# Building a graph's adjacency blocks: a fixed window of 20 targets per tile, or 12 targets placed from the data

## The chip, the cores and the metric

The kernel runs on one core of a Trainium2 chip, in one launch. The metric is the device time of that core in microseconds (us). Five engines work side by side, each with its own instruction queue: TensorE (PE in the profile, its weight loads PEld), VectorE (DVE), ScalarE (ACT), GpSimd (POOL) and the DMA-issuing SyncE (SP).

## The reference, cut to what matters

A graph of 625 nodes with 512 features and 20,000 edges, sorted by target node `dst`, goes through four message-passing layers, each `x = x + layer(relu(norm(x)))`. The first two need, for each target, a sum over its edges:

```python
# layer 0: a mean of neighbours
neighbor_sum   = segment_sum(h[src], dst, n)
neighbor_count = segment_sum(ones, dst, n)
# layer 1, twice: 4 bases, 8 edge types
m   = sum_b comp[etype, b] * (h @ basis[b])[src]
agg = segment_sum(m * edge_weight, dst, n)
```

The edges are the same in both layers, so the sums are products with matrices that are built once: `cnt` (how many edges go from source to target) and eight weighted matrices `adj` (two sublayers, four bases), each 625 x 625.

## The kernel before, in words

The edges lie in 160 tiles of 125 (`NT`, `P`), in order of target. A tile's targets are near 625/160 = 3.9 times its number (`PACE`), give or take 8 (`SLACK`). The prologue in `tile_gnn` tests that for every edge; the number of offenders, `n_far`, selects the ordered body or a general one.

In the ordered body, `layers01_near` builds the matrices before any layer runs. First `coefficients` forms, in three calls of four, four and two slices, each edge's eight coefficients, and splits each into three bf16 parts whose sum is the f32 value; with a constant one for the count that is 25 columns per edge (`parts`). Then 20 steps (`s`) take eight tiles each, in two halves of four (`G`):

- VectorE makes `eq`, for each tile a comparison of its targets with the 20 (`W`) from a fixed start `low[t]`, and multiplies it with the 25 columns into `rh` (L441): 4 x 25 x 20 elements per half.
- VectorE makes `ohs` (L450), a one-hot of the tile's sources over five chunks of 128.
- TensorE multiplies them, for each tile five chunks by three parts (L455), into five PSUM tiles `q`, one per chunk, at the tile's offset. Eight PSUM tiles exist, so a step needs two that the step before has to give back.
- The windows of neighbouring steps overlap. VectorE adds the overlapping columns into `adj` and `cnt` (L466); ScalarE copies the new columns (L467).

After step 0 the loads of `x` and of later weights are queued (`load_rest`, `layer2_weights`); at steps 10 and 11 `x` is normalised (`norm_stats`, `norm_relu`). Then layer 0 starts with transposes of `h` (L213), the counts `pc` (L491) and the neighbour sums (L502). The order within an engine is that of a scheduler, except where `keep` pins an instruction behind the one before it on its engine.

Of the kernel before, what the change touches and what calls it, by code (L numbers as in the profile page):

```python
# [9 lines left out]
F32 = mybir.dt.float32  # L10
F16 = mybir.dt.float16
I32 = mybir.dt.int32
AF = mybir.ActivationFunctionType
# [17 lines left out]
SILU_2MOM = 1.679177  # L31
PACE = P * N / E
SLACK = 8


def locals_of(v):
    return [v[k] for k in "src_i dst_i src_f dst_f ew ea4 x iota_f ident ones eps two row iota_s rel_no mine et_r comp".split()]


@with_exitstack  # L40
def tile_gnn(ctx: ExitStack, tc: tile.TileContext, a: dict, out: bass.AP):
    nc = tc.nc
    const = ctx.enter_context(tc.tile_pool(name="const", bufs=1))

    with tc.tile_pool(name="temp", bufs=1) as temp:
        src_i = const.tile([P, NT], I32, name="src_i")
        dst_i = const.tile([P, NT], I32, name="dst_i")
        ew = const.tile([P, NT], F32, name="ew")
# [57 lines left out]
        nc.vector.reduce_sum(mine, blk, axis=mybir.AxisListType.X)  # L106


        dst_f = const.tile([P, NT], F32, name="dst_f")
        nc.vector.tensor_copy(dst_f, dst_i)  # L110
        off = temp.tile([P, NT], F32, name="off")
        nc.vector.scalar_tensor_tensor(off, tile_f, -PACE, dst_f, op0=ALU.mult, op1=ALU.add)
        out_lo = temp.tile([P, NT], F32, name="out_lo")
        nc.vector.tensor_scalar(out_lo, off, -float(SLACK), None, op0=ALU.is_lt)
        nc.vector.tensor_scalar(off, off, PACE + SLACK, None, op0=ALU.is_gt)
        nc.vector.tensor_add(off, off, out_lo)
        n_out = const.tile([P, 1], F32, name="n_out")
        nc.vector.reduce_sum(n_out, off, axis=mybir.AxisListType.X)
        far = const.tile([1, 1], I32, name="far")
        with tc.tile_pool(name="flag", bufs=1, space=bass.MemoryType.PSUM) as fp:  # L120
            pf = fp.tile([128, 512], F32, name="pf")
            nc.tensor.matmul(pf[:1, :1], n_out, ones, start=True, stop=True)
            nc.vector.tensor_copy(far, pf[:1, :1])
        src_f = const.tile([P, NT], F32, name="src_f")
        nc.vector.tensor_copy(src_f, src_i)
        nc.vector.tensor_copy(iota_s, src_no)
        n_far = nc.values_load(far, min_val=0, max_val=E)
    with tc.If(n_far < 1) as ordered:
        gnn_body(tc, a, out, locals_of(locals()), True)
    with ordered.Else():  # L130
# [13 lines left out]
def gnn_body(ctx: ExitStack, tc: tile.TileContext, a: dict, out: bass.AP, consts, near: bool):  # L144

    nc = tc.nc
    (src_i, dst_i, src_f, dst_f, ew, ea4, x, iota_f, ident, ones, eps, two, row, iota_s, rel_no,
     mine, et_r, comp) = consts
    sfx = "n" if near else "g"
    node = ctx.enter_context(tc.tile_pool(name=f"node{sfx}", bufs=1))  # L150
    work = ctx.enter_context(tc.tile_pool(name=f"work{sfx}", bufs=2))
# [227 lines left out]
    def layers01_near(wts2):  # L379
# [1 line left out]


        NQ = 2 * NB
        W = 20
        NS = NT // (2 * G)
        BF16 = mybir.dt.bfloat16
        low = [min(max(math.ceil(t * PACE - SLACK), 0), N - W) for t in range(NT)]
        with tc.tile_pool(name="adjacency", bufs=1) as bp:
            adj = bp.tile([P, NC, NQ, N], F32, name="adj")
            with tc.tile_pool(name="counts", bufs=1) as cp:  # L390
                cnt = cp.tile([P, NC, N], F32, name="cnt")
                with tc.tile_pool(name="build", bufs=2) as lp, \
                        tc.tile_pool(name="ps_build", bufs=8, space=bass.MemoryType.PSUM) as pp:

                    T = 128 // R
                    K = NT // T
                    cd = lp.tile([128, T, NQ], F32, name="cd", bufs=1)
                    nc.vector.tensor_mul(cd, mine[:, :, None].to_broadcast([128, T, NQ]),  # L400
                                         comp.rearrange("p l b -> p (l b)")[:, None, :].to_broadcast([128, T, NQ]))
                    oh_r = lp.tile([128, K, P], F32, name="oh_r", bufs=1)

                    parts = lp.tile([P, NT, 3 * NQ + 1], BF16, name="parts", bufs=1)
                    nc.gpsimd.memset(parts[:, :, NQ:NQ + 1], 1.0)
                    by_k = parts.rearrange("p (t k) q -> p k t q", k=K)
                    ew_k = ew.rearrange("p (t k) -> p k t", k=K)
                    keep = tc.keep_in_program_order

                    def coefficients(k0):  # L410
                        ks = slice(k0, min(k0 + 4, K))
                        n = ks.stop - k0
                        keep(nc.vector.tensor_scalar(oh_r[:, ks, :], et_r[:, ks, :], rel_no, None,
                                                     op0=ALU.is_equal))
                        p = pp.tile([128, 4, T, NQ], F32, tag="q", name="pco")
                        for k in range(n):
                            nc.tensor.matmul(p[:P, k], oh_r[:, k0 + k, :], cd, start=True, stop=True)
                        co = lp.tile([P, 4, T, NQ], F32, tag="co", name="co")[:, :n]
                        keep(nc.vector.tensor_mul(co, p[:P, :n],
                                                  ew_k[:, ks, :, None].to_broadcast([P, n, T, NQ])))  # L420
                        for i in range(3):
                            q0 = i * NQ + (i > 0)
                            v = by_k[:, ks, :, q0:q0 + NQ]
                            keep(nc.vector.tensor_copy(v, co))
                            if i < 2:
                                keep(nc.vector.tensor_sub(co, co, v))

                    coefficients(0)
                    end = 0
                    for s in range(NS):  # L430
                        b0 = low[s * 2 * G]
                        wd = low[(s + 1) * 2 * G - 1] + W - b0
                        q = [pp.tile([128, NQ + 1, 48], F32, tag="q", name="q") for _ in range(NC)]
                        for i in range(2):
                            eq = lp.tile([P, G, W], BF16, tag="eq", name="eq")
                            rh = lp.tile([P, G, 3 * NQ + 1, W], BF16, tag="rh", name="rh", bufs=3)
                            t0 = (2 * s + i) * G
                            for j in range(G):
                                nc.vector.tensor_scalar(eq[:, j, :], iota_f[:, low[t0 + j]:low[t0 + j] + W],
                                                        dst_f[:, t0 + j:t0 + j + 1], None, op0=ALU.is_equal)  # L440
                            keep(nc.vector.tensor_mul(  # L441
                                rh, eq[:, :, None, :].to_broadcast([P, G, 3 * NQ + 1, W]),
                                parts[:, t0:t0 + G, :, None]
                                .to_broadcast([P, G, 3 * NQ + 1, W])))
                            if s == 0:
                                coefficients(4 + 4 * i)
                            for j in range(G):
                                t = t0 + j
                                os_ = lp.tile([P, NC, 128], BF16, tag="ohs", name="ohs", bufs=6)
                                nc.vector.tensor_scalar(os_, iota_s, src_f[:, t:t + 1], None, op0=ALU.is_equal)  # L450
                                o = low[t] - b0
                                for c in range(NC):
                                    for k in range(3):
                                        q0, n = k * NQ + (k > 0), NQ + (k == 0)
                                        nc.tensor.matmul(q[c][:, :n, o:o + W], os_[:, c, :],  # L455
                                                         rh[:, j, q0:q0 + n, :],
                                                         start=i + j + k == 0,
                                                         stop=i == 1 and j == G - 1 and k == 2,
                                                         skip_group_check=True)

                        old = max(end - b0, 0)
                        for c in range(NC):
                            for dst, v in ((adj[:, c, :, b0:b0 + wd], q[c][:P, :NQ, :wd]),
                                           (cnt[:, c, None, b0:b0 + wd], q[c][:P, NQ:, :wd])):
                                if old:
                                    nc.vector.tensor_add(dst[:, :, :old], v[:, :, :old], dst[:, :, :old])  # L466
                                nc.scalar.copy(dst[:, :, old:], v[:, :, old:])  # L467
                        end = b0 + wd
                        if s == 0:
                            load_rest()  # L470
                            w2s = layer2_weights(wts2)
                        if s == NS // 2:
                            h = node.tile([P, NC, D], F32, tag="h", name="h")
                            stats = [norm_stats(c, keep) for c in range(NC)]
                        if s == NS // 2 + 1:
                            for c in range(NC):
                                norm_relu(h, c, stats[c], keep)
# [1028 lines left out]
```

## Time and profile before

| | us |
|---|---|
| median of three runs (1879.14 to 1885.42) | 1883.51 |
| the profiled execution, its own time | 1883.0 |
| its span in the profile | 1881.2 |
| PE busy over the span | 1772.1 (94%) |
| DVE busy over the span | 1074.1 (57%) |
| POOL busy over the span | 809.9 (43%) |
| first product of step 0 to first product of step 1 | 21.68 to 34.58 |
| first product of step 19 | 211.28 |
| first transpose of layer 0 | 221.42 |

The shares over the span mix stages with different limits. The adjacency build is the stretch up to about 220 us; what a change to it is worth has to be read from that stretch.

### The profile page before, as it was taken

Reading aid. Unit: us, or ns where it says so; the run is one execution under the profiler, and the core shown is the slowest. Engines: PE = TensorE matmul, PEld = TensorE weight load, DVE = VectorE, ACT = ScalarE, POOL = GpSimd, SP = SyncE. Lnnn points to the kernel's source line nnn. Section 1 sums busy time; section 2 is a strip of 40 time slices with the busy share of each in tenths; the row PEclk is TensorE's granted clock in tenths of the full one; section 3 lists DMA queues with packets and bytes.
Section 4 is the critical chain, followed back from the end, with each engine's and each line's share of the span. In section 5 each row is a group of like instructions: output and inputs, shape, how many; then the busy total and the mean of one; then the engine's idle time right before and its main releaser. Section 6 shows DMA issues by size and latency. Waiting matters only on the chain.

```text
span 1881.2 us, 25801 instructions
## 1 busy us (share of the span) xinstructions
PE 1772.1 (94%) x10688; PEld 960.7 (51%) x10688; DVE 1074.1 (57%) x1877; ACT 741.3 (39%) x856; POOL 809.9 (43%) x478
## 2 busy tenths in 40 slices
PE   5999999999999999999999989999999999999993
PEld 5999844444444444445455444444454444545441
DVE  8999611001100267768774657786676676666655
ACT  1122211000000312222221766767776777668670
POOL 0000000000000077556543688888887888788200
PEclk9999999999999989999999989999999999999996
DMA  2000103003000176565443589666675666666200
GB/s 70 2 2 2 52 0 140 0 0 93 2 0 0 30 187 162 139 146 161 125 119 98 116 150 172 127 122 119 109 132 114 115 132 116 109 119 125 36 0 13
DMA packets 157223, 162.68 MB, mean 86 GB/s; under 512 B 97546, under 2 KB 104059, under 8 KB 157096
## 3 DMA queue, kind: packets, MB, share of 16 engines
q0 software_dynamic: 131584, 119.48, 32.4%
q1 hardware_dynamic: 20100, 32.69, 5.7%
q10 hardware_dynamic: 5412, 8.77, 1.7%
q8 instruction: 86, 1.41, 0.3%
q14 instruction: 41, 0.34, 0.1%
HBM read 155.11 MB, written 5.12 MB: 85 GB/s over the span
## 4 chain that ended last, share of the span: by engine, by line
PE 83%; DVE 11%; ACT 2%; DMA 2%; issue 1%; POOL 0%; DVEq 0%; SPq 0%; ACTq 0%; POOLq 0%
PE z L1243 29%; PE agg L557 9%; PE hb L544 7%; PE sum L856 7%; PE tpw L834 5%; DVE rh L441 4%; PE z L1224 4%; PE z L1229 4%; DVE ohs L450 2%; PE agg L1267 2%; PE xsd L932 2%; PE mlp L786 2%; PE agg L533 2%; PE l L509 2%; PE nsum L502 1%
## 5 line engine op out<-in xcount | busy, mean ns | idle before, releaser
L1243 PE MATMUL z<-wm,z 128*125 128x512 f32 x1280 | 556.9, 593 | 2.7 <-DVE z L1362 2.7
L1243 PEld LDWEIGHTS z<-wm,z 128*125 128x125 f32 x1280 | 237.5, 188 | 293.5 <-issue 268.8
L230 POOL DMA_INDIRECT g_s<-xs,src_i x160 | 303.4, 1896 | 126.1 <-issue 75.5
L230 POOL DMA_INDIRECT g_s<-xd,dst_i x144 | 300.6, 2087 | 43.9 <-issue 42.0
L798 POOL MEMSET mT<- 128x5000 f32 x1 | 4.3, 4267 | 633.4 <-PE agg L557 633.4
L230 POOL DMA_INDIRECT gup<-up,src_i x160 | 198.1, 1238 | 132.0 <-DVE msg L841 60.6
L455 PE MATMUL q<-rh,ohs 125*128 125x160 bf16 (+1 forms) x2400 | 184.5, 238 | 13.5 <-ACT cnt L467 11.0
L455 PEld LDWEIGHTS <-ohs 125*128 125x128 bf16 x2400 | 180.0, 99 | 17.8 <-issue 15.0
L1245 DVE TENSOR_TENSOR mess<-z,b 125x512 f32<-125x512 f32 x160 | 106.4, 687 | 136.4 <-PE z L1243 136.4
L557 PE MATMUL agg<-hb,adj 125*125 125x512 f32 x400 | 173.6, 592 | 0.0
L547 DVE COPY hb<-hb 125x512 f32<-125x512 f32 x20 | 13.8, 692 | 261.0 <-PE hb L544 261.0
L856 PE MATMUL sum<-msg,ohy 125*32 125x128 f32 (+1 forms) x2560 | 146.0, 303 | 8.5 <-issue 6.9
L841 DVE TENSOR_TENSOR msg<-tpw,gup 125x768 f32<-125x768 f32 x160 | 152.0, 950 | 0.0
L856 PEld LDWEIGHTS sum<-msg,ohy 125*32 125x32 f32 x2560 | 101.2, 109 | 86.7 <-issue 85.7
L1231 DVE TENSOR_SCALAR z<-z,b 128x500 f32<-128x500 f32 (+1 forms) x164 | 108.4, 719 | 59.4 <-PE z L1229 57.5
L544 PE MATMUL hb<-basis,hT 128*125 128x512 f32 x320 | 138.6, 592 | 0.0
L1191 ACT ACTIVATE uz<-uz 128x2000 f32<-128x2000 f32 (+1 forms) x41 | 75.0, 1830 | 153.0 <-DVE uz L1183 153.0
L557 PEld LDWEIGHTS agg<-hb,adj 125*125 125x125 f32 x400 | 74.8, 188 | 94.7 <-issue 94.7
L549 ACT COPY hb<-hb 125x512 f32<-125x512 f32 x20 | 11.7, 586 | 258.3 <-PE hb L544 238.4
L839 DVE TENSOR_TENSOR msg<-tpw,gup 125x256 f32<-125x256 f32 x160 | 67.0, 419 | 62.9 <-PE tpw L834 31.1
L1191 ACT ACTIVATE um<-um 125x2048 f32<-125x2048 f32 x39 | 74.6, 1912 | 71.1 <-DVE um L1183 71.1
L544 PEld LDWEIGHTS hb<-basis,hT 128*125 128x125 f32 x320 | 60.1, 188 | 77.3 <-issue 76.8
(187 smaller groups left out, 2240.5 us busy)
## 6 DMA issues: line engine op xcount, KB each, us to landing
rt<-in_edge_attr SPq DMA_DIRECT2D x76, 125.0 KB
basis<-in_L_gnn_basis SPq DMA_DIRECT2D x8, 1024.0 KB
gup<-up,src_i POOLq DMA_INDIRECT x160
g_s<-xs,src_i POOLq DMA_INDIRECT x160
g_s<-xd,dst_i POOLq DMA_INDIRECT x144
w<-in_L_gnn_W SPq DMA_DIRECT2D x2, 1024.0 KB
loop<-in_L_gnn_loop SPq DMA_DIRECT2D x2, 1024.0 KB
w1ab<-in_L_gnn_W ACTq DMA_DIRECT2D x1, 2048.0 KB
```

Source lines behind the costliest of these rows:

```text
L230: return nc.gpsimd.indirect_dma_start(out=dst, out_offset=None, in_=table, in_offset=bass.IndirectOffsetOnAxis(ap=idx[:, t:t + 1], axis=0) ...
L441: keep(nc.vector.tensor_mul(rh, eq[:, :, None, :].to_broadcast([P, G, 3 * NQ + 1, W]), parts[:, t0:t0 + G, :, None] .to_broadcast([P, G, 3 ...
L455: nc.tensor.matmul(q[c][:, :n, o:o + W], os_[:, c, :], rh[:, j, q0:q0 + n, :], start=i + j + k == 0, stop=i == 1 and j == G - 1 and k == 2 ...
L544: nc.tensor.matmul(p[:P, :], hT[:, k, s * P:(s + 1) * P], basis[b][:, k, :], start=k == 0, stop=k == KD - 1)
L557: nc.tensor.matmul(acc[c], adj[:, s - 1, l * NB + b, c * P:(c + 1) * P], hb[:, b, :], start=False, stop=s == NC and b == NB - 1)
L834: nc.tensor.matmul(p[:P, :], hid[s // 2][s % 2][rws, i * P:(i + 1) * P], w4[rws].rearrange("p k u -> p (k u)"), start=True, stop=True)
L841: nc.vector.tensor_mul(m[:, :, 1:, :], pv[:, 2:4, None, :].to_broadcast([P, 2, 3, MUL]), g[:, None, 1:, :].to_broadcast([P, 2, 3, MUL]))
L856: nc.tensor.matmul(A[r * W:(r + 1) * W, c * MUL:c * MUL + v.shape[1]], oh[:, j, q, :], v, start=j % G == 0 and r not in done, stop=j % G = ...
L1191: keep(nc.scalar.activation(u, u, AF.Exp))
L1231: keep(nc.vector.tensor_scalar(zv[:, n, f, :], pf[f][:, :ne], b1[:, f:f + 1], None, op0=ALU.add))
L1243: nc.tensor.matmul(p[:P, :], z[:, j // w, f, j % w * P:(j % w + 1) * P], wm2[:, f, :], start=f == 0, stop=f == KD - 1)
L1245: keep(nc.vector.tensor_add(m[:, j, :], p[:P, :], bc["b2"]))
```

## The change

Twelve targets per tile in place of 20. Each group of eight tiles gets a base, worked out in the prologue from the target of the first edge of its fifth tile; a tile's 12 targets start at the base plus four (`STEP`) times its place in the group, so a group spans 40 targets (`WS`). Positions relative to that start (`rel`) are kept in a free part of `x`, and edges that fall outside the 12 are counted into `n_far` too. Two short products share one PSUM pool there.

Since the base is data, a step's 40 columns are written at an address from a register. `adj` and `cnt` are zeroed first (GpSimd: `cnt` and chunks 0 to 2; ScalarE: chunks 3 and 4), and every step is added in place. ScalarE copies `q` to `got` in SBUF and GpSimd adds it, for all five chunks in even steps; in odd steps VectorE adds chunks 3 and 4 from PSUM itself. The adding of a step is queued in the middle of the next. The comparisons `eq` are made for many tiles at once (`hots`). Of the one-hots of sources five are kept in place of six.

```diff
+NS = NT // (2 * G)
+STEP = 4
+WT = 12
+WS = (2 * G - 1) * STEP + WT
...
+        nc.tensor.matmul(pb[:, :NS], top, by_s[:, :, G], start=True, stop=True)
+        nc.vector.tensor_sub(rel, by_s, step_f)
...
+        nc.vector.tensor_scalar(base_f, pb[:, :NS], -float(STEP * G + (WT - STEP) // 2), 0.0,
+                                op0=ALU.add, op1=ALU.max)
+        nc.vector.tensor_scalar_min(base_f, base_f, float(N - WS))
+        nc.vector.tensor_copy(base_i, base_f[:1, :])
+        nc.vector.tensor_sub(rel, rel, base_f[:P, :, None].to_broadcast([P, NS, 2 * G]))
+        flat_rel = rel.rearrange("p s j -> p (s j)")
+        nc.vector.scalar_tensor_tensor(off, flat_rel, 0.0, off, op0=ALU.is_lt, op1=ALU.add)
+        nc.vector.scalar_tensor_tensor(off, flat_rel, WT - 1.0, off, op0=ALU.is_gt, op1=ALU.add)
...
-        low = [min(max(math.ceil(t * PACE - SLACK), 0), N - W) for t in range(NT)]
...
+                    def hots(t0, t1):
+                        keep(nc.vector.tensor_tensor(
+                            eq[:, t0:t1, :], iota_f[:, None, :WT].to_broadcast([P, t1 - t0, WT]),
+                            flat_rel[:, t0:t1, None].to_broadcast([P, t1 - t0, WT]), op=ALU.is_equal))
+
+                    hots(0, G)
+                    keep(nc.gpsimd.memset(cnt, 0.0))
+                    keep(nc.gpsimd.memset(adj[:, :3], 0.0))
+                    for c in range(3, NC):
+                        keep(nc.scalar.activation(adj[:, c], iota_f[:, None, :].to_broadcast([P, NQ, N]),
+                                                  AF.Copy, scale=0.0))
...
+                    def moved(s, eng):
+                        loads, (at,) = nc.values_load_multi_w_load_instructions(
+                            base_i[:1, s:s + 1], engines=(eng,), min_val=0, max_val=N - WS,
...
+                    def added(s):
+                        q = done.pop(s)
+                        lo, hi = STEP * (s == NS - 1), WS - STEP * (s == 0)
+                        n = NC - 2 * (s % 2)
+                        got = lp.tile([P, NC, NQ + 1, WS], F32, tag="got", name="got")[:, :n]
+                        for c in range(n):
+                            nc.scalar.copy(got[:, c, :, lo:hi], q[c][:P, :, lo:hi])
+                        at = moved(s, mybir.EngineType.Pool)
+                        for dst, v in ((adj[:, :n, :, at][:, :, :, lo:hi], got[:, :, :NQ, lo:hi]),
+                                       (cnt[:, :n, at][:, :, lo:hi], got[:, :, NQ, lo:hi])):
+                            keep(nc.gpsimd.tensor_add(dst, v, dst))
+                        if n < NC:
+                            at = moved(s, mybir.EngineType.DVE)
+                        for c in range(n, NC):
+                            for dst, v in ((adj[:, c, :, at][:, :, lo:hi], q[c][:P, :NQ, lo:hi]),
+                                           (cnt[:, c, at][:, lo:hi], q[c][:P, NQ, lo:hi])):
+                                keep(nc.vector.tensor_add(dst, v, dst))
...
-                            for j in range(G):
-                                nc.vector.tensor_scalar(eq[:, j, :], iota_f[:, low[t0 + j]:low[t0 + j] + W],
-                                                        dst_f[:, t0 + j:t0 + j + 1], None, op0=ALU.is_equal)
...
-                                os_ = lp.tile([P, NC, 128], BF16, tag="ohs", name="ohs", bufs=6)
...
-                        old = max(end - b0, 0)
-                        for c in range(NC):
-                            for dst, v in ((adj[:, c, :, b0:b0 + wd], q[c][:P, :NQ, :wd]),
-                                           (cnt[:, c, None, b0:b0 + wd], q[c][:P, NQ:, :wd])):
-                                if old:
-                                    nc.vector.tensor_add(dst[:, :, :old], v[:, :, :old], dst[:, :, :old])
-                                nc.scalar.copy(dst[:, :, old:], v[:, :, old:])
...
+                                hot.append(lp.tile([P, NC, 128], BF16, tag="ohs", name="ohs", bufs=5))
+                                nc.vector.tensor_scalar(hot[j], iota_s, src_f[:, 2 * s * G + j:2 * s * G + j + 1],
+                                                        None, op0=ALU.is_equal)
+
+                                if j == 1:
+                                    for cs in (range(3), range(3, NC)):
+                                        counted(0, cs)
+                                        counted(1, cs)
+                                elif j > 1:
+                                    counted(j, range(NC))
+                            if i == 0 and s > 0:
+                                added(s - 1)
+                        if s == NS - 1:
+                            added(s)
```

`rh` and the products are as before with 12 in place of 20: `rh` has 4 x 25 x 12 elements per half, the products 108 and 96 columns in place of 180 and 160.

## The prediction

> **What bounds the kernel now.** I read the page first. TensorE is busy nearly everywhere, so its share says nothing about a single stage; the rows of slices do (40 slices of 47 us). In slices 2 to 4 VectorE is at 8 or 9 tenths as well, and GpSimd is idle until slice 14.
>
> ```profile
> PE   5999999999999999999999989999999999999993
> DVE  8999611001100267768774657786676676666655
> POOL 0000000000000077556543688888887888788200
> ```
>
> That stretch is the adjacency build. The busy time of each engine in a window inside it, and the groups of instructions by shape up to 340 us:
>
> ```profile
> 85.00:125.00 40.00, 37.25 (x492) 36.38 (x490) 39.35 (x120) 8.19 (x41) 0.00 (x0) 1.00 0.01 2
> L455 PE MATMUL q<-rh,ohs 125*128 125x160 bf16 x1600 | 181.8, 236 | 0.0
> L455 PE MATMUL q<-rh,ohs 125*128 125x180 bf16 x800 | 179.3, 243 | 13.5 <-ACT cnt L467 11.0 <-DVE rh L441 2.4
> L441 DVE TENSOR_TENSOR rh<-eq,parts 125x2000 bf16<-125x2000 bf16 x40 | 89.4, 2237 | 0.1
> L450 DVE TENSOR_SCALAR ohs<-iota_s,src_f 125x640 bf16<-125x640 f16 x160 | 54.9, 382 | 0.3
> L439 DVE TENSOR_SCALAR eq<-iota_f,dst_f 125x20 bf16<-125x20 f32 x160 | 27.5, 232 | 0.0
> L466 DVE TENSOR_TENSOR adj<-q,adj 125x128 f32<-125x128 f32 x75 | 18.8, 286 | 3.9 <-PE q L455 3.9
> ```
>
> VectorE has no gap (39.35 of 40 us, clock 1.00 throughout), TensorE is close behind. In the chain of waits ordinary steps alternate rh, ohs, eq and the adds of L466: VectorE carries them. One step in the timeline:
>
> ```profile
> 55.16 8.82 PE L455 MATMUL q<-rh,ohs 125*128 125x180 bf16 x119 [0.65 <-ACT cnt L467]
> 57.63 2.24 DVE L441 TENSOR_TENSOR rh<-eq,parts 125x2000 bf16<-125x2000 bf16 x1
> 59.78 0.97 DVE L450 TENSOR_SCALAR ohs<-iota_s,src_f 125x640 bf16<-125x640 f16 x3
> 64.76 8.89 PE L455 MATMUL q<-rh,ohs 125*128 125x180 bf16 x119 [0.78 <-ACT cnt L467]
> ```
>
> Steps start 9.6 us apart here, 9.86 at most among plain ones; I take 9.7. TensorE streams 120 products at 8.82/119 = 74 ns and then waits 0.65 to 0.8 us for PSUM that VectorE and ScalarE still hold. By start-to-start distance VectorE's step is two rh of 2.15, eight ohs of 0.297, eight eq of 0.141, and ten adds with their gaps, 1.8: 4.3 + 2.4 + 1.1 + 1.8 = 9.6. It is full by itself.
>
> **The change, part by part.**
>
> *It takes the ordered body still.* The reference's own edges, put through the new arithmetic, give relative positions from exactly 0 to exactly 11: no edge is outside, n_far stays 0.
>
> *VectorE's step.* rh falls to 1200 elements; 2.15 us for 2000 is 1.04 ns each plus 0.07, so 1.31, two are 2.6. The ohs stay at 2.4. eq is gone from the step. Even steps: 5.0 us. In odd ones VectorE also adds two chunks: 320 elements each (256 to 320 on the same engine: about 0.40 apart) and 40 (0.12), 1.05 in all, and loads a register. The nearest row is the load of n_far, 0.55 us on its queue; with restart 0.7. Behind it stand rh and four ohs, and TensorE behind these. 6.75 us; mean 5.9.
>
> *TensorE's step.* 100 columns on average in place of 167. In proportion 74 ns become 44, 5.3 us a step. The weight loads are the other end: 50 products of one f32 column (L491) take 117 ns each, transposes of 125 columns (20 in 2.33 us) also 117, so that is the load of f32 weights, and an f32 column costs twice a bf16 one (512 in 435 ns on L1243 against 167 in 74), so about 58 for one bf16 pass. I take 55: 6.6 us. The Trainium skill, "TensorE: Matmul & The Clock Gate", section "Back-to-back issue gap", puts a stream of load and product pairs at about 81 ns at 128 columns, which would make it 9.7 and end the gain here; the trace has 74 at 167 columns, so the rule is too high for this stream.
>
> *ScalarE's step.* Five copies of 360 elements, under 0.5 each (0.475 for 320): 2.5 us, idle otherwise; its two zeroings of 5000 elements, by L1191 (1.83 for 2000) some 4.6 each, lie before its first copy, which starts at 34.0 now. Nothing on the path.
>
> *GpSimd's step.* New: 1600 + 200 elements (even), 960 + 120 (odd), and a register load. No addition by GpSimd is in the trace. Its memset of 5000 f32 is the nearest row:
>
> ```profile
> L798 POOL MEMSET mT<- 128x5000 f32 x1 | 4.3, 4267 | 633.4 <-PE agg L557 633.4
> ```
>
> 0.85 ns an element for one stream. An addition has two reads and a write: 1.7 if a read hides the write, 2.6 if nothing hides. The skill's "GPSIMD Engine Reference", section "Elementwise — side-by-side cycle accounting", has 4497 ns for 2048, 2.2 ns, between them. 4.15 and 2.55 us with 0.1 per instruction; alone it fits beside VectorE.
>
> *The port.* It is not alone. Two places show VectorE and GpSimd in each other's way:
>
> ```profile
> 9.67 0.82 POOL L405 MEMSET parts<- 125x160 bf16 x1 [6.37 <-DVE far L123]
> 10.02 0.74 DVE L413 TENSOR_SCALAR oh_r<-x,rel_no 128x500 f32<-128x500 int32 x1
> 19.29 0.48 DVE L413 TENSOR_SCALAR oh_r<-x,rel_no 128x500 f32<-128x500 int32 x1
> ...
> 1403.72 1.24 POOL L230 DMA_INDIRECT g_s<-xs,src_i  x1 [0.30 <-PE z L1229]
> 1405.07 1.20 DVE L1183 TENSOR_SCALAR uz<-z 128x2000 f32<-128x2000 f32 x1
> 1405.27 2.11 POOL L230 DMA_INDIRECT g_s<-xs,src_i  x1 [0.30 <-issue]
> ```
>
> The same oh_r takes 0.26 us longer beside a memset, and ends 0.27 after it; a gather takes 0.87 longer when it starts beside a VectorE instruction that has 0.9 to go. The skill says why, "SBUF — State Buffer", section "Who interferes with whom": the pair of ports is held for a whole instruction, against GpSimd by single-input VectorE instructions in a two-port mode (ohs at 0.3 us for 640 elements, oh_r, the casts) and, where GpSimd reads, by those with two SBUF inputs (rh). Adds from PSUM are free of it. So by the rule nearly all of VectorE's step and all of GpSimd's exclude each other: 5.0 + 4.15 = 9.15 even, about 8.4 odd (the register load and adds go beside GpSimd), mean 8.8. Without contention the step is TensorE's 6.6, say 6.7. I take 8.2: nearer the rule, since two rows show it, but not at it, since in the gathers only GpSimd waits (L1183 never exceeds 1.26 us), and[...] the statistics of step 10 can run meanwhile. Gain: 19 x (9.7 - 8.2) = 28.5.
>
> *Step 0.* rh twice 0.84 less, eq 1.7 less (step 1's too), hots 2.3 more (1920 elements): 1.0 less. But GpSimd now zeroes 3125 + 15000 elements, by L798 2.7 + 12.8 us, one instruction of 12.8, while VectorE stands before oh_r, casts and ohs. Bounds: 0, if long memsets yield; 13, if held to the end. The row of oh_r shows a hold to the end, but of under half a microsecond. No row shows a long one; I take 6. Behind the stalled VectorE stand rh and all of TensorE.
>
> *Prologue.* About eight small instructions more on the path to n_far: three of 0.33, a subtraction of 0.3, a conversion, a minimum and a read of PSUM of 0.15 to 0.2: 1.9. All queues wait for that branch.
>
> *Tail.* After the last product now 2.4 us to the transposes, 4.6 to the counts pc. Then: three copies 1.2, GpSimd 2.6, 0.3 of latency, 4.1 to pc, the transposes before it: nothing, up to 2 more if GpSimd is late. The load of L0's weights, issued at 220.01 once the build's memory is free, has until about 254, when nsum ends; that cover is enough.
>
> Sum against the profiled 1883.0 (0.5 below the median of the runs shown): -28.5 - 1.0 + 6 + 1.9 = -21.6, so **1861.4**.
>
> **The rivals.**
>
> *Hardly any contention.* GpSimd takes its turns in the gaps; steps at 6.7. 19 x 3.0 = 57, plus 1.0, less 1.9 and up to 6: -50 to -56, about 1829.[...] Against: the rows above.
>
> *TensorE keeps its pace.* If weight loads keep 74 ns, the step is 8.9 whatever VectorE does: 19 x 0.8 = 15, less 1.9 and 0 to 6, plus 1.0: -8 to -14, about 1872. Against: the mean of 58 above.
>
> *The held port turns it slower.* In step 0 the memset holds VectorE for the full 13, and the additions cost 2.6 ns an element: 1440 a step are 3.75 + 0.2, VectorE 5.0 and 0.3 beside them, 9.25. 19 x 0.45 = 8.6 gained against 13 + 1.9 - 1.0: +5.3, and 1890 with the tail. It decides where 19 times the step's saving falls below 14: at steps over 8.96. At the skill's 2.2 ns (8.8) the full hold leaves about -3, no change.
>
> **How the numbers follow.** The turn-taking forecast (-10 to -35) has 0.43, little contention (-35 to -57) 0.20, TensorE at its old pace 0.07; the full hold 0.30, of which 0.10 within 0.3% (5.6 us, about what can be told from no change here) and 0.20 slower. Faster 0.70, same 0.10, slower 0.20. The range leaves out 0.1 on each side: 1829 to 1893. The likeliest case alone: 1848 to 1873.
>
> **What would show it.** The distance of first products of neighbouring steps: 8.2, against 6.7 or 9.3. Right for the port: ohs or rh far longer than 0.38 and 1.4 when they start beside a GpSimd addition. Step 0: oh_r or an ohs of many microseconds beside the memset of adj; first product of step 1 at about 41, not 35 or 47. GpSimd's addition of 1600: 2.8 to 4.3 us. TensorE's product pace in a burst: 44 to 58 ns. Wrong would be a wait of TensorE for GpSimd in plain steps, or odd steps longer than even ones by more than 1 us (a register load dearer than 0.7).

## The result, and the profile after

The changed kernel takes 1881.99 us (median of 20 runs, 1878.88 to 1891.12) against 1887.32 (20 runs, 1879.14 to 1898.46): ratio 0.9981, 95% interval 0.997 to 0.9992. By that ratio, which is of the means, it is 3.6 us shorter where 22 were forecast; the medians differ by 5.3. The profiled execution took 1885.24, its span is 1883.4.

The rows of slices of the page:

```profile
PE   2777899999999989999999989999999999999993
DVE  8999520001000267777674657786676676666665
POOL 4444200000000176555543588888887888788200
```

In slices 2 to 4 VectorE is as full as before and TensorE no longer is, at 7 tenths. GpSimd works now where it was idle. The groups of the build, by shape (busy us in all, mean ns of one, then the engine's idle time before them and what ended it):

```profile
L514 PE MATMUL q<-rh,ohs 125*128 125x108 bf16 x800 | 125.1, 223 | 48.4 <-DVE ohs L529 35.4 <-DVE rh L521 12.5 <-ACT got L493 0.5
L529 DVE TENSOR_SCALAR ohs<-iota_s,src_f 125x640 bf16<-125x640 f16 x160 | 84.0, 575 | 3.5 <-PE q L514 3.3
L521 DVE TENSOR_TENSOR rh<-eq,parts 125x1200 bf16<-125x1200 bf16 x40 | 69.3, 1737 | 0.1
L497 POOL TENSOR_TENSOR adj<-got,adj 125x1600 f32 x9 | 31.0, 3446 | 47.6 <-issue 40.7 <-ACT got L493 6.9
L497 POOL TENSOR_TENSOR adj<-got,adj 125x960 f32 x9 | 19.7, 2191 | 41.0 <-ACT got L493 41.0
```

The ohs have the same shape as before, where one took 382 ns and all 160 took 54.9 us; now the mean is 575 and the sum 84.0. TensorE waits 35.4 us for them, which it did not before. One place in the timeline, an even step's addition:

```profile
113.89 5.57 PE L514 MATMUL q<-rh,ohs 125*128 125x108 bf16 x120 [1.79 <-DVE ohs L529]
118.39 3.33 POOL L497 TENSOR_TENSOR adj<-got,adj 125x1600 f32 x1 [6.91 <-ACT got L493]
118.47 4.06 DVE L529 TENSOR_SCALAR ohs<-iota_s,src_f 125x640 bf16<-125x640 f16 x2
121.96 0.27 PE L514 MATMUL q<-rh,ohs 125*128 125x108 bf16 x1 [2.50 <-DVE ohs L529]
```

Two ohs that take 0.67 otherwise last 4.06: they begin 0.08 after GpSimd's addition and end after it, and TensorE stands for 2.5 us. A whole step of 120 products takes TensorE only 5.57 us. And step 0:

```profile
11.71 0.82 POOL L435 MEMSET parts<- 125x160 bf16 x1 [8.04 <-DVE far L157]
12.10 3.04 POOL L468 MEMSET cnt<- 125x3125 f32 x1
12.19 15.76 DVE L444 TENSOR_SCALAR oh_r<-x,rel_no 128x500 f32<-128x500 int32 x1
15.07 12.60 POOL L469 MEMSET adj<- 125x15000 f32 x1
27.87 1.55 DVE L529 TENSOR_SCALAR ohs<-iota_s,src_f 125x640 bf16<-125x640 f16 x5
```

One oh_r, 0.74 us before, takes 15.76: it ends 0.28 after the memset of adj, and VectorE does nothing else in that time.

Where the time went, by marks of the timelines: the first product of step 1 and the first transpose of layer 0, before (L455, L213) and after (L514, L247).

```profile
34.58 10.33 PE L455 MATMUL q<-rh,ohs 125*128 125x180 bf16 x133 [1.06 <-DVE rh L441]
221.42 2.33 PE L213 MATMUL tr<-ident,h 125*128 125x125 f32 x20 [1.49 <-ACT cnt L467]
53.98 9.51 PE L514 MATMUL q<-rh,ohs 125*128 125x108 bf16 x180 [6.44 <-DVE rh L521]
215.63 2.33 PE L247 MATMUL tr<-ident,h 125*128 125x125 f32 x20 [1.15 <-DVE cnt L503]
```

The first product of step 1 moves from 34.58 to 53.98, 19.4 later. From there to the first transpose of layer 0 a step takes (215.63 - 53.98)/19 = 8.51 us on average, before (221.42 - 34.58)/19 = 9.83 (both with the statistics of step 10 in them): 25.2 shorter in all. So the transposes start 5.8 earlier. What follows them is the same code in both kernels; it took 1659.8 us before and 1667.8 after in the profiled executions. Most of those 8 us is the scatter of single executions: the profiled one before lies 4.3 below its kernel's median, that of the change 3.3 above. In the eight profiles a1 to a5 and b1 to b3 below that stretch took 1649 to 1664.

### The profile page after: what moved, and what is told of

It reads as the page before. It is cut to its first block, busy times and chain, and to the rows that moved or that the text cites. A ratio compares the mean times of both kernels' runs of the same rounds, so it can differ in the third digit from the quotient of the medians.

```text
span 1883.4 us, 25706 instructions
## 1 busy us (share of the span) xinstructions
PE 1724.4 (92%) x10690; PEld 910.3 (48%) x10690; DVE 1068.2 (57%) x1582; ACT 739.8 (39%) x738; POOL 899.8 (48%) x521
## 4 chain that ended last, share of the span: by engine, by line
PE 84%; DVE 8%; issue 3%; DMA 2%; ACT 1%; POOL 0%; DVEq 0%; ACTq 0%; POOLq 0%; SPq 0%
PE z L1316 29%; PE agg L630 9%; PE hb L617 7%; PE sum L929 7%; PE tpw L907 5%; PE z L1302 4%; PE z L1297 4%; PE q L514 3%; DVE ohs L529 2%; PE agg L1340 2%; PE xsd L1005 2%; PE agg L606 2%; PE l L582 2%; PE mlp L859 2%; PE nsum L575 1%
## 5 line engine op out<-in xcount | busy, mean ns | idle before, releaser
L264 POOL DMA_INDIRECT g_s<-xs,src_i x160 | 297.8, 1861 | 127.5 <-issue 76.1
L264 POOL DMA_INDIRECT g_s<-xd,dst_i x144 | 307.2, 2133 | 43.9 <-issue 41.7
L514 PE MATMUL q<-rh,ohs 125*128 125x96 bf16 (+1 forms) x2400 | 127.7, 220 | 48.4 <-DVE ohs L529 35.4
L514 PEld LDWEIGHTS <-ohs 125*128 125x128 bf16 x2400 | 123.7, 105 | 52.4 <-DVE ohs L529 38.3
L622 ACT COPY hb<-hb 125x512 f32<-125x512 f32 x20 | 11.7, 585 | 260.0 <-PE hb L617 240.0
L497 POOL TENSOR_TENSOR adj<-got,adj 125x960 f32 (+3 forms) x20 | 55.8, 2789 | 114.8 <-ACT got L493 74.1
```

Source lines behind the costliest of these rows:

```text
L264: return nc.gpsimd.indirect_dma_start(out=dst, out_offset=None, in_=table, in_offset=bass.IndirectOffsetOnAxis(ap=idx[:, t:t + 1], axis=0) ...
L514: nc.tensor.matmul(q[c][:, :n, o:o + WT], hot[j][:, c, :], rhs[j // G][:, j % G, q0:q0 + n, :], start=j + k == 0, stop=j == 2 * G - 1 and ...
```

## The experiments

Theory 1: VectorE and GpSimd exclude each other for whole instructions at their shared ports, in step 0 and in every addition. Theory 2: the two only coincide; oh_r waits for something else, and the step is set by the five one-hots that tie VectorE to TensorE. Step times below are taken as above, by the first product of step 1, the first transpose and a division by 19.

| run | step 1 starts | transposes start | step | us | before beside it |
|---|---|---|---|---|---|
| before | 34.58 | 221.42 | 9.83 | | |
| the change | 53.98 | 215.63 | 8.51 | | |
| a1_zero_scalar | 41.88 | 203.88 | 8.53 | 1865.82 | 1880.40 |
| a2_zero_pieces | 45.65 | 206.52 | 8.47 | 1870.18 | 1880.40 |
| a3_adds_vector | 51.64 | 200.84 | 7.85 | 1857.95 | 1880.40 |
| a5_no_pool_adds | 42.58 | 156.28 | 5.98 | 1819.25 | 1880.40 |
| a4_both | 40.26 | 188.98 | 7.83 | 1853.27 | 1881.28 |
| b1_pool_add | 36.70 | 283.33 | 12.98 | 1934.38 | 1881.28 |
| b2_pool_memset | 37.41 | 259.64 | 11.70 | 1917.85 | 1881.28 |
| b3_w12 | 33.41 | 179.94 | 7.71 | 1845.85 | 1881.28 |
| a6_all_zero_scalar | 36.64 | 185.39 | 7.83 | 1820.37 | 1852.70 |
| a7_split_two | 36.46 | 171.05 | 7.08 | 1803.21 | 1852.70 |

The last two ran on another chip, where the kernel before takes 1852.70; they are compared with that.

**Zeroing by ScalarE (a1_zero_scalar).**

```diff
-                    keep(nc.gpsimd.memset(adj[:, :3], 0.0))
-                    for c in range(3, NC):
+                    for c in range(NC):
                         keep(nc.scalar.activation(adj[:, c], iota_f[:, None, :].to_broadcast([P, NQ, N]),
```

> The changed kernel, with all five chunks of adj zeroed by ScalarE; GpSimd keeps only cnt. Theory 1 (GpSimd holds the shared ports for a whole instruction): the first oh_r, 15.8 us now, waits only for the memset of cnt, so about 3.3 us; step 1 starts near 41.4 in place of 54.0, and the whole is about 12.6 us shorter, 1869. ScalarE zeroes until about 35 (13.0 + 5 x 4.36), before its first copy. Theory 2 (oh_r waits for its own data, the stall only coincides with the memset): oh_r stays near 15 us and the time stays at 1882.

Measured: ratio to before 0.9913 (0.9889 to 0.9936). The same lines of its timeline:

```profile
11.99 3.03 POOL L468 MEMSET cnt<- 125x3125 f32 x1
12.08 3.22 DVE L444 TENSOR_SCALAR oh_r<-x,rel_no 128x500 f32<-128x500 int32 x1
```

oh_r ends 0.28 after the memset of cnt, as it did after that of adj. Step 1 starts 12.1 earlier, the step is unchanged (8.53). Theory 2 has no account of this.

**Zeroing in pieces (a2_zero_pieces).**

```diff
-                    keep(nc.gpsimd.memset(cnt, 0.0))
-                    keep(nc.gpsimd.memset(adj[:, :3], 0.0))
+                    for c in range(NC):
+                        keep(nc.gpsimd.memset(cnt[:, c], 0.0))
+                    for c in range(3):
+                        for b in range(NQ):
+                            keep(nc.gpsimd.memset(adj[:, c, b], 0.0))
```

> The changed kernel, with the same zeroing on GpSimd cut into 5 pieces for cnt and 24 for adj, 625 elements each, about 0.55 us a piece. Theory 1 with a hold per instruction: oh_r waits for one piece, under 1.3 us, later VectorE instructions for one piece each, and step 1 starts near 43. Theory 1 with a hold that passes from one GpSimd instruction to the next when they follow without a gap: oh_r stays at 15 us or more, as if it were one memset. Theory 2: 15 us as well, but then the first run's oh_r is 15 too.

Measured, one run: 1870.18, step 1 at 45.65. Its timeline:

```profile
12.27 3.99 POOL L469 MEMSET cnt<- 125x625 f32 x5
12.36 1.14 DVE L444 TENSOR_SCALAR oh_r<-x,rel_no 128x500 f32<-128x500 int32 x1
13.41 3.77 DVE L532 TENSOR_SCALAR ohs<-iota_s,src_f 125x640 bf16<-125x640 f16 x5
```

The hold is per instruction: oh_r is through after 1.14, and five ohs take 3.77 in place of 1.55, about half a microsecond lost at each. In the changed kernel oh_r stood through the ends of two GpSimd memsets before its turn came, so at such an end the next queued GpSimd instruction can win as well.

**Additions by VectorE (a3_adds_vector).**

```diff
-                        n = NC - 2 * (s % 2)
-                        got = lp.tile([P, NC, NQ + 1, WS], F32, tag="got", name="got")[:, :n]
-                        for c in range(n):
-                            nc.scalar.copy(got[:, c, :, lo:hi], q[c][:P, :, lo:hi])
-                        at = moved(s, mybir.EngineType.Pool)
...
-                            keep(nc.gpsimd.tensor_add(dst, v, dst))
+                        n = 0
```

> The changed kernel, with every step added by VectorE from PSUM (no copies by ScalarE, no additions by GpSimd); the zeroing is as in the changed kernel. Theory 1: no instruction of VectorE meets a GpSimd one after step 0, so no rh over 1.42 and no ohs over 0.40; a step is 5.0 + a register load 0.7 + 5 x (0.40 + 0.11) = 8.2 us, against 8.67 now: 9 us shorter in all, about 1873, while oh_r in step 0 stays at 15.8. Theory 2 (the step is set by the five one-hots and by TensorE's coupling to VectorE, not by the ports): the step gets longer by what VectorE is given, to 10 us or more, and the whole is 20 us longer.

Measured, one run: 1857.95, step 7.85. Giving VectorE more work made the step shorter, against theory 2. oh_r keeps its 15.76, no ohs exceeds 0.388 and no rh 1.409 us. The forecast of 1873 was too long: the transposes start 14.8 earlier than in the change, not 9, and the rest is the scatter of what follows them.

**No additions (a5_no_pool_adds).** With the edit of a1, and after step 0 nothing is added by GpSimd:

```diff
-                            keep(nc.gpsimd.tensor_add(dst, v, dst))
+                            if s == 0:
+                                keep(nc.gpsimd.tensor_add(dst, v, dst))
```

> The kernel of the first run, with GpSimd's additions left out after step 0 (the matrices are therefore incomplete in eight of ten chunks); copies, register loads and VectorE's own adds of odd steps stay. Theory 1: the step falls from 8.67 to VectorE's own, 5.0 in even and up to 6.8 in odd steps, or TensorE's 5.6 plus its waits: 6.2 on average; with the zeroing moved the whole is 12.6 + 18 x 2.4 = 56 shorter than the changed kernel, about 1826. Theory 2: the step stays over 8 us.

Measured, one run: 1819.25, step 5.98. Its groups:

```profile
L521 DVE TENSOR_TENSOR rh<-eq,parts 125x1200 bf16<-125x1200 bf16 x40 | 55.9, 1402 | 0.1
L529 DVE TENSOR_SCALAR ohs<-iota_s,src_f 125x640 bf16<-125x640 f16 x160 | 51.8, 376 | 3.4 <-PE q L514 3.0
```

Beside the changed kernel's 69.3 and 84.0, these two groups alone are 45.6 us shorter. The one-hots are still five here, so it isn't they that set the step of the change. Beside a1, which zeroes in the same way, GpSimd's additions cost 8.53 - 5.98 = 2.55 us a step.

**Both edits (a4_both).** The diffs of a1 and a3 together.

> The changed kernel with both edits: ScalarE zeroes adj, and VectorE adds every step from PSUM. Theory 1: the gains add up, 12.6 from step 0 and about 9 from the steps, 1860, unless VectorE's register loads and adds cost more than 3.2 us a step. Theory 2: no faster than the changed kernel.

Measured: ratio 0.9848 (0.9824 to 0.9872), 1853.27. The gains add up, and more, since the step is 7.83 and not 8.2. A whole step of its timeline, here the two ends of it, shows why:

```profile
100.00 0.48 DVE L495 TENSOR_TENSOR adj<-q,adj 125x320 f32 x1
...
106.34 1.26 DVE L521 TENSOR_SCALAR ohs<-iota_s,src_f 125x640 bf16<-125x640 f16 x4
107.52 0.48 DVE L495 TENSOR_TENSOR adj<-q,adj 125x320 f32 x1
107.92 0.19 DVE L495 TENSOR_TENSOR cnt<-q,cnt 125x40 f32 x1
```

From one step's first add to the next one's are 7.52 us, and in them VectorE has no gap: two rh and eight ohs fill 5.00, ten adds 2.52. The register load, forecast at 0.7, shows nowhere. (The step in the table is longer by the statistics and the end of the build.)

**A useless addition in the kernel before (b1_pool_add).**

```diff
+                    pad = lp.tile([P, NC, NQ, 39], F32, name="pad", bufs=1)
+                    keep(nc.gpsimd.memset(pad, 0.0))
...
+                        keep(nc.gpsimd.tensor_add(pad, adj[:, :, :, b0:b0 + 39], pad))
                         end = b0 + wd
```

> The kernel before, with one addition on GpSimd per step that is of no use: 1560 f32 of adj into a scratch tile, about 3.4 us, which nothing waits for except the next step's adds. Theory 1: VectorE, full at 9.6 us, loses the addition's whole duration, so a step is about 13 us and the kernel 20 x 3.3 = 65 longer, 1950. Theory 2 (ports cost little, the changed kernel's step is set otherwise): the step stays within 0.5 us of 9.8.

Measured, one run: 1934.38, step 12.98. From its timeline and its groups:

```profile
114.19 3.30 POOL L470 TENSOR_TENSOR pad<-adj,pad 125x1560 f32<-125x1560 f32 x1 [9.47 <-ACT cnt L469]
114.40 3.27 DVE L452 TENSOR_SCALAR ohs<-iota_s,src_f 125x640 bf16<-125x640 f16 x1
L443 DVE TENSOR_TENSOR rh<-eq,parts 125x2000 bf16<-125x2000 bf16 x40 | 101.2, 2532 | 0.1
L470 POOL TENSOR_TENSOR pad<-adj,pad 125x1560 f32<-125x1560 f32 x20 | 66.8, 3341 | 207.5 <-ACT cnt L469 207.5
```

An addition of 3.34 makes the step 3.15 longer. Nothing else of the change is in this kernel, and it isn't a wait for the sums: from step 1 to the transposes 56.7 of the 59.8 us more are time in which VectorE's own instructions last longer. rh suffers too, 101.2 in place of 89.4. The total grew by 53 and not 65; the transposes start 61.9 later, and the rest is the scatter of what follows them.

**Useless memsets in the kernel before (b2_pool_memset).**

```diff
+                    pad = lp.tile([P, 2000], F32, name="pad", bufs=1)
...
+                        for _ in range(2):
+                            keep(nc.gpsimd.memset(pad, 0.0))
+                        tiny = lp.tile([P, 1], F32, tag="tiny", name="tiny")
+                        keep(nc.scalar.copy(tiny, pad[:, :1]))
                         end = b0 + wd
```

> The kernel before, with two memsets of 2000 elements on GpSimd per step that are of no use, 1.7 us each, paced by a one-column copy on ScalarE. They write and read nothing. If a writer stops only single-input VectorE instructions in a two-port mode, rh runs at 2.24 beside it and ohs or eq wait: a loss between 0 (it falls beside rh) and 3.4 a step. If it stops rh as well, the step grows by the full 3.4, to 13. If ports cost little, no change.

Measured, one run: 1917.85, step 11.70, 1.87 longer. From its timeline and its groups:

```profile
102.90 3.84 POOL L470 MEMSET pad<- 125x2000 f32 x2 [8.68 <-ACT tiny L472]
103.04 1.83 DVE L440 TENSOR_SCALAR eq<-iota_f,dst_f 125x20 bf16<-125x20 f32 x2
L442 DVE TENSOR_TENSOR rh<-eq,parts 125x2000 bf16<-125x2000 bf16 x40 | 89.2, 2233 | 0.3
```

A memset stops even an eq of 20 elements, but never rh: 13 of the 40 lie beside one, at 2.23 us like the others. So it costs less than its length, by how much of it falls beside rh.

**The narrowing alone (b3_w12).**

```diff
-        W = 20
+        W = 12
```

> The kernel before with a window of 12 fixed targets per tile in place of 20, and nothing else changed (edges outside the 12 are left out of the matrices). This is the change's narrowing alone, without registers, zeroing or additions in place. VectorE: two rh of 1.31, eight ohs 0.297, eight eq 0.14, adds 1.8: 7.9 us a step by theory 1 and 2 alike, TensorE 5.6: 19 x 1.8 = 34 shorter than before, about 1850. If TensorE's wait for PSUM at the step's start or the longer chain of L466 and L467 sets the step, 8.5 or more.

Measured, one run: 1845.85, step 7.71, 35 us shorter than before. That is what the narrower window is worth with the old way of adding, in a kernel that leaves out the edges outside the 12. The change has the same window, and its transposes start 35.7 later than here: 20.6 by a later step 1 (53.98 against 33.41) and 19 x 0.80 = 15.2 by longer steps.

**All zeroing on ScalarE (a6_all_zero_scalar)** and **two chunks for GpSimd in every step (a7_split_two).** Both zero all of adj and cnt by ScalarE; the first adds as a4 does, the second with

```diff
-                        n = NC - 2 * (s % 2)
+                        n = 2
```

> The kernel with both edits, with cnt zeroed by ScalarE too, so that GpSimd touches nothing but the parts memset of 0.8 us during the build. Theory 1: the first oh_r falls from 3.2 us to about 0.9, and the rest is as with both edits: 2.5 shorter, 1851. ScalarE's zeroing ends near 38, about when the first add of VectorE wants it; if it is late, step 1 waits up to 1.5 us and the gain is 1.

> All zeroing on ScalarE, and in every step GpSimd adds chunks 0 and 1 (640 + 80 elements, about 1.4 + 0.3 us) while VectorE adds chunks 2 to 4 from PSUM, which needs no shared port. Theory 1: if the two adds lie beside each other, VectorE loses nothing to the hold and its step is 5.0 + 0.7 + 3 x 0.51 = 7.2 us, against 7.8 with VectorE alone: 1840. If GpSimd's adds fall beside rh or ohs all the same, as those of odd steps did in part, the hold of 1.7 is lost and the step is 8.9 at the worst, 1872.

Measured: ratio 0.982 (0.9799 to 0.9841), and 0.9732 (0.971 to 0.9754). Both are faster than the kernel before by more than the change is (0.9981). The longest oh_r takes 0.61 and 0.62 us. In a7 the step is 7.08:

```profile
116.97 0.48 DVE L503 TENSOR_TENSOR adj<-q,adj 125x320 f32 x1
117.11 1.45 POOL L497 TENSOR_TENSOR adj<-got,adj 125x640 f32 x1 [11.18 <-ACT got L493]
117.36 0.19 DVE L503 TENSOR_TENSOR cnt<-q,cnt 125x40 f32 x1
117.47 2.35 DVE L521 TENSOR_TENSOR rh<-eq,parts 125x1200 bf16<-125x1200 bf16 x1
```

VectorE's adds from PSUM go on beside GpSimd's addition at 0.48 and 0.19, their free lengths. Of its 60 adds into adj, 50 lie beside a GpSimd addition, at 0.473 us on average, and the others take 0.476. What is left of the addition is lost at rh, 2.35 in place of 1.40.

## Why the prediction was wrong

The mechanism was named and the sign was right. The term that failed is the hold in step 0: 6 us forecast, 17.7 measured.

- **Step 0** was put at 6, between 0 and 13. The hold was total: oh_r took 15.0 longer, since VectorE stood through the end of the memset of parts and both of the others. The 13 was not even the upper end, though the same paragraph had the 2.7 us for cnt. GpSimd's first addition, which the forecast of step 0 did not hold, then stretched a cast from 0.31 to 3.00. Together these are 17.7, of the 19.4 by which step 1 is later. a1 gets back 12.1 of it by one edit.
- **In the sum**: 11.7 more in step 0, 3.3 less gained in the steps (25.2, forecast 28.5) and 0.8 in the prologue and the rest of step 0 turn the forecast of -21.6 into -5.8, by which the transposes start earlier.
- **The port** in the steps was put at 8.2. Counted on VectorE, from the first rh of a step to that of the next, plain steps behind step 1 took 9.61 before and take 8.22 now (16 of them, 7.05 to 9.11). The table's 8.51 holds the statistics and the end of the build as well. So the number was right by luck, since its reason was not. The 3.3 less gained come from a step before of 9.61 and not 9.7, and from what lies outside the plain steps. The reason for going below the rule, that in the gathers only GpSimd waits, did not carry over: in b1 VectorE loses 3.15 of 3.34 us. And the rule's 8.8 was itself too high: if the odd steps' adds and register load lie beside GpSimd, as the forecast said, its terms give 5.0 + 2.55 = 7.55 there and not 8.4. With the sizes measured where undisturbed (VectorE 5.00; GpSimd 3.33 + 0.66 in even steps, 2.07 + 0.49 in odd ones) the rule gives 8.99 and 7.56, an estimate of 8.28 on average.
- So the rule of the Trainium skill's "SBUF — State Buffer", section "Who interferes with whom", held here in the parts that were tried: a whole instruction is waited for (a1, a2), two SBUF inputs collide with an addition (b1) and not with a memset (b2), and adds from PSUM go free (a7).
- The rival of the full hold had "about -3, no change" at 2.2 ns an element. It was the case that came; it had 0.30 in the chances, 0.10 of it for no change. That its -3 lies so near the 3.6 is luck in part: it had 13 for step 0, which was 17.7, and 8.8 for the step.
- **The prologue**: 1.9 forecast; VectorE's first instruction of the body starts at 11.86 in place of 9.81, 2.05.
- **VectorE's own step**: rh of 1.40 and ohs of 0.376 as forecast in a5. The register load was put at 0.7; no gap is seen for it in a4. So the steps of a3 and a4 were forecast at 8.2, about 0.35 too long.
- **TensorE**: 5.57/120 = 46 ns a product, near the end of the forecast that goes by columns, 44, and not at 55. The 81 ns that the skill's "TensorE: Matmul & The Clock Gate", section "Back-to-back issue gap", has for such pairs at 128 columns do not hold for this stream of 100. It didn't matter, as VectorE was late.
- **GpSimd's addition**: 3.32 us for 1600 and 2.07 for 960 where undisturbed, so (3.32 - 2.07)/640 = 1.95 ns an element and 0.2 for the instruction; forecast 2.2 and 0.1.
- **The tail**: the transposes come 1.15 after the last product instead of 1.49 (idle time before them), and its products wait for none of its weights. But pc, 5.86 us before, takes 7.79. This was not in the sum.

Left open is what makes the 2 us between the transposes' 5.8 and the 3.6 of the ratio: pc alone could be all of it, and the scatter of what follows is larger.

## What to carry to other kernels

Before work moves to GpSimd, look at what VectorE does beside it. Casts and one-hots like those here stand still for the whole of a GpSimd instruction that began first, and those with two operands in SBUF (rh) do if it reads as well: add the two times, and look for long memsets in a stretch where GpSimd was idle before. Put beside a GpSimd addition what VectorE reads from PSUM, and zero large tiles by ScalarE or in pieces. When a change has several parts, price the part that pays by itself: here the narrower window was worth 35 us (b3), and what placing it from the data needs, the zeroing, the additions and a longer prologue, took all but 4 of them back.

## What was not expected of the hardware

The stretch behind the build is not granted the same clock in every kernel. Here it is from the transposes to the end of pc, with the granted clock third from the end, before, after and in b3_w12:

```profile
221.00:230.00 9.00, 8.58 (x71) 8.56 (x72) 0.35 (x3) 2.68 (x6) 0.00 (x0) 0.91 0.75 261
215.50:226.00 10.50, 10.37 (x71) 10.39 (x72) 0.04 (x1) 2.50 (x5) 2.05 (x2) 0.74 0.59 217
180.00:193.00 13.00, 13.00 (x69) 13.00 (x69) 0.00 (x0) 2.69 (x5) 0.00 (x0) 0.54 0.47 172
```

The same 70 instructions (20 transposes, 50 products of pc) take longer where the clock is lower. These are the counts pc, before and after, from the chains of waits:

```profile
223.75 5.86 PE pc L491 x50
217.96 7.79 PE pc L564 x50
```

In b3_w12 they take 10.50 us.

What sets the clock there stays open. It is tempting to blame TensorE's waits in the build, where it was granted 0.92 between 60 and 170 us and 1.00 before, but the runs do not bear that out. In the last 20 us of the build a4 and a6 (on two chips) are alike, with TensorE busy for 14.35 and 14.36 us and a clock of 1.00; in the 9 us behind it they are granted 0.83 and 0.57. a5 keeps TensorE busier there, 18.88 of 20 at 1.00, and gets 0.78.
